# A routed-experts kernel on one core: another order of 21 tiles, and GpSimd in the manual schedule

## The chip, the core and the metric

The kernel runs on one core of one Trainium2 chip. The metric is the device time of one execution in microseconds, as a median of several runs. One execution was also taken with the hardware profiler; durations in this text are from it, unless they are called medians of the runs.

## The reference

The input x has 16 rows of 512 tokens with 128 channels, in float32. Every token is normalized, and three things are added up: x itself, a linear attention with decay, and a mixture of four experts of which each token takes two.

```python
xn = layernorm(x)                                   # (16, 512, 128)
# attention: 32 channels, no softmax, a token looks at those after it
scores = einsum('btc,bsc->bts', xn @ q_w, xn @ k_w) * decay_weights
att = (einsum('bts,bsc->btc', scores, xn @ v_w) @ o_w.T) * out_scale
# experts
rw, sel = top_k(xn @ router_w + router_b + load_balancer, 2); rw = softmax(rw)
e0 = (silu(xn @ sw_w1) * (xn @ sw_w3)) @ sw_w2      # hidden width 512
e1 = gelu(((xn @ eq + b) @ wv + b) @ wo @ c1w + b) @ c2w + b     # 256
syn = xn @ syn_w + b
h2 = layernorm(syn + (syn @ wv + b) @ wo + b) * n1g + n1b
e2 = (layernorm(h2 + relu(h2 @ f1w + b) @ f2w + b) * n2g + n2b) @ gen_w + b
e3 = gelu(xn @ ml_w1 + b) @ ml_w2 + b               # 512
out = x + att + rw[0] * e[sel[0]] + rw[1] * e[sel[1]]
```

## The kernel before

**Rows.** Each of the 16 rows (512 tokens, four chunks of 128) is loaded, its moments are taken on VectorE (`stats`), the reciprocal root on GpSimd (`inv`, L484), the normalization on ScalarE (`norm`, L494), a transpose and a projection to q, k, v and router logits on TensorE (`turn`, `proj`). Four rows make a `Quad`, for which the attention is computed together: `keys`, `score`, `scored` (L659), `near`, `far`, `outputs`, and `total` (L718), which adds the result to x; then the row is stored to the output in HBM (L602).

**Lists.** Rows are routed in groups (`GROUPS`, 2, 2, 4, 4 and 4 rows). There is one list in HBM for each pair of experts, six in all. When a group is routed, GpSimd scatters its tokens with their weights and numbers to the lists by indirect DMAs, one for each chunk (`send`, L506, destination `lists`, 64 in all).

**Tiles.** A list is then worked off in tiles of up to four chunks: `LISTS` gives the pair and the chunks of its tiles. A tile is loaded from the list on SyncE's queue (`L`, L880), transposed (`T`, `TT`), its biases are written to an accumulator `o` on VectorE (`B`, L908 and L910), and the two experts of its pair are computed. Expert 0 is `ga`, `gb` (a_ps, b_ps), experts 1 and 3 are `H` (h_ps) and an activation on ScalarE (`A`, L939), expert 2 has two normalizations with a turn of z after each (`U`, `S`, `I`, `O`, `N`, `Zu`, `F`, `Zv`). `Y` is each expert's last product (y_ps), `J` adds it by weight to `o` on VectorE (L963). Finally GpSimd adds `o` to the output by an indirect DMA for each chunk (`X`, L506, destination `out_dram`, 66 in all). Each X waits for all 16 row stores. There are four buffers `o`, four `xg`, three `xT`, and one each of `h0`, `h1`, `h3`.

**The order.** No loop of the code runs in this order. All steps are put into a plan with `add`: engine, a cost in us, what they wait for, which buffers they take until when, and a rank. `emit` goes through it like a list scheduler: it looks for the step that can start first, and of those on the same engine that can start within 0.25 us of it, takes the one of the lowest rank. The order that comes out is written as the program, and the manual schedule keeps it on its engines. The ranks are 5 for each row, 12 for each tile, in the order of `TURN`, and the offsets in `AHEAD`:

```python
rank = 5.0 * (b + QUAD - 1) + AHEAD["quads"][b // QUAD]     # attention of the quad of row b
rank = 5.0 * b - AHEAD["rows"] - (120.0 if b < 2 else 0.0)  # row b
tiles[pair, i].steps(k, g, AHEAD["tiles"] + 12.0 * k)       # k-th tile of TURN
```

`TURN` names a tile (pair, number) and the group after whose scatters it may be loaded. Should a list have fewer tokens by then than the tile takes, or more at the end than its tiles hold, the flag `turns` lets a loop at the end compute all rows densely instead. The last three tiles (`LAST`) are joined in parts of half a tile. Constant products (`fill`, `busy`) keep TensorE going while it has nothing else.

Of the kernel before, what the change touches and what calls it, by code (L numbers as in the profile page):

```python
# [11 lines left out]
ALU = mybir.AluOpType  # L12
# [5 lines left out]
P = 128  # L18
# [8 lines left out]

LISTS = [
    ((0, 1), (3, 4, 4, 4)), ((0, 2), (3, 2)), ((0, 3), (4, 4)),
    ((1, 2), (3, 3, 4, 3)), ((1, 3), (2, 4, 3, 4, 4, 3)), ((2, 3), (3, 2)),  # L30
]
NL = len(LISTS)
LR = 16 * 512
# [2 lines left out]


TURN = [
# [4 lines left out]
]  # L43
FILL = 25

AHEAD = {"rows": -2.0, "tiles": 62.0, "biases": -5.0, "quads": (9.0, -36.0, -27.0, -27.0)}
LAST = 3


# [39 lines left out]
def decay_attention__plus__routed_experts(  # L89
# [10 lines left out]
    nc = tc.nc  # L100
# [37 lines left out]
    def buf(pool, kind, shape, name, by):  # L138

        tag = kind if pool is once else f"{kind}.{which(kind, by)}"  # L140
        return pool.tile(shape, F32, tag=tag, name=f"{kind}_{name}", bufs=1)

    lists = tc.dram_tile([NL * LR, PW], F32, name="lists")


    queue = {"on": False, "fixed": None, "moving": []}
    behind = mybir.DependencyInfo(mybir.DependencyClass.NoSync, mybir.DependencyReason.DATA)

    def queued(i, key=None):

        if queue["on"]:
            others = [q for q, k in queue["moving"] if k != key or key is None]
            for q in others or [queue["fixed"]]:
                if q is not None:
                    tc.add_manual_dep(i.ins, q, behind, reason="the order of the plan")
            if key:
                queue["moving"].append((i.ins.name, key))
            else:
                queue.update(fixed=i.ins.name, moving=[])
        return i  # L160

    def mm(o, lhsT, rhs, start=True, stop=True):
        nc.tensor.matmul(o, lhsT, rhs, start=start, stop=stop)  # L163
# [6 lines left out]
    plan = {}  # L170
# [113 lines left out]
    neg_half = const.tile([P, NC], F32, tag="neg_half", name="neg_half")  # L284
# [27 lines left out]

    def bounds():
        for l, (pair, sizes) in enumerate(LISTS):
            queued(nc.gpsimd.memset(limit[:, l : l + 1], float(l * LR + P * sum(sizes))))
            for g in range(NG):
                last = max((k for q, k, at in TURN if q == pair and at <= g < NG - 1), default=-1)
                queued(nc.gpsimd.memset(need[:, g, l : l + 1], float(l * LR + P * sum(sizes[: last + 1]))))

    limit = const.tile([P, NL], F32, tag="limit", name="limit")  # L320

    need = const.tile([P, NG, NL], F32, tag="need", name="need")
# [101 lines left out]
    d_col = const.tile([P, 1], F32, tag="d_col", name="d_col")  # L424
    d_far = const.tile([P, 1], F32, tag="d_far", name="d_far")
# [10 lines left out]
    add("d_col", V, 0.15, lambda: nc.vector.tensor_scalar(d_col, d_col, 0.5, 0.5, ALU.mult, ALU.add), ["d_tanh"], rank=-97.0)  # L436

    def squared():
        queued(nc.gpsimd.tensor_tensor(d_far, d_col, d_col, ALU.mult))
        for _ in range(6):  # L440
            queued(nc.gpsimd.tensor_tensor(d_far, d_far, d_far, ALU.mult))

    add("d_far", G, 1.9, squared, ["d_col"], rank=-95.0)
    add("powers", V, 0.5, lambda: nc.vector.tensor_tensor_scan(
        powers, d_col.to_broadcast([P, P + 1]), one, 0.0, ALU.mult, ALU.add), ["d_col"], rank=-95.0)
# [35 lines left out]

    def inverse(ve, n, pool, name):
        rstd = pool.tile([P, n], F32, tag=f"rstd{name[0]}", name=f"rstd_{name}", bufs=FEW.get(name[0], 1))
        queued(nc.gpsimd.tensor_tensor(rstd, ve, neg_half[:, :n], ALU.pow))  # L484
        return rstd

    def offset(mv, rstd, n, pool, name):
# [15 lines left out]

    def scatter(o, src, index, n, key, **how):

        i = queued(nc.gpsimd.indirect_dma_start(  # L506
            out=o, out_offset=bass.IndirectOffsetOnAxis(ap=index, axis=0),
            in_=src, in_offset=None, bounds_check=n - 1, oob_is_err=False, **how,
        ), key)
        tc.add_to_no_dep_group(key, i.ins)  # L510
        tc.declare_no_dep(i.ins, group=key, reason="each row of the table is written once at most")
        if key == "lists":
            tc.declare_no_dep(i.ins, group="loads", reason="a tile is loaded when all its rows are there")
# [47 lines left out]
    class Row:  # L561
# [8 lines left out]
        def inv(s):  # L570
            s.rstd = inverse(s.ve, NC, small, f"x_{s.b}")
# [148 lines left out]
    class Group:  # L720
# [5 lines left out]
        def number(s):  # L726
            s.pay = [buf(work, f"pay{s.m}", [P, NC * s.m, PW], f"{s.g}_{k}", running[0]) for k in range(s.n // (NC * s.m))]
            for k, pay in enumerate(s.pay):
                at = NC * (s.first + s.m * k)
                number = tok[:, at : at + NC * s.m].unsqueeze(2).to_broadcast([P, NC * s.m, PW - P - 2])  # L730
                queued(nc.gpsimd.tensor_copy(pay[:, :, P + 2 :], number))

        def entry(s, k):
            return s.pay[k // (NC * s.m)][:, k % (NC * s.m), :]
# [39 lines left out]
        def send(s, k):  # L774
            scatter(lists, s.entry(k), s.idx[:, k : k + 1], NL * LR, "lists")

    quads = []

    def attention(b, a):

        rank = 5.0 * (b + QUAD - 1) + AHEAD["quads"][b // QUAD]
        of = range(QUAD)
# [23 lines left out]
    for g, m in enumerate(GROUPS):  # L806
        q = Group(g, first, m)
        q.before, before = before, q
        add(f"tok{g}", G, 0.25, q.number, takes=[(f"pay{q.m}", [f"send{g}.{NC * q.m * i + k}" for k in range(NC * q.m)]) for i in range(m // q.m)], at=6.0, rank=-200.0)
        for b in range(first, first + m):  # L810
            k = NC * (b - first)
            r = Row(b, work, lambda c, k=k, q=q: q.entry(k + c)[:, :D])
            lg = q.lg[:, :, k : k + NC]
            rank = 5.0 * b - AHEAD["rows"] - (120.0 if b < 2 else 0.0)
            ends = [f"store{b}"]
# [29 lines left out]
            if b % QUAD == QUAD - 1:  # L845
                attention(q0, quads[-1])
        rank = 5.0 * (first + m) - AHEAD["rows"] - 50.0
        n = NC * m
# [7 lines left out]
        for k in range(n):  # L856
# [3 lines left out]
            add(f"send{g}.{k}", G, 1.28, lambda q=q, k=k: q.send(k), need_q, rank=rank + 20.0)  # L860
        first += m
    add("bounds", G, 1.3, bounds, ["send0.3"], rank=0.0)


# [3 lines left out]
    class Tile:  # L868
# [110 lines left out]
        def inv(s, key):  # L979
            s.rstd = inverse(s.ve, s.n, s.tmp, f"{key}_{s.name}")  # L980
# [29 lines left out]
        def send(s, c):  # L1010
            scatter(rows_of_out, s.o[:, c, :], s.to[:, c : c + 1], B * T, "out", compute_op=ALU.add)

        def steps(s, k, g, ranks):
# [6 lines left out]
            def step(q, eng, us, fn, after=(), takes=(), rank=0.0):  # L1020
                add(name(q), eng, us, fn, [name(a) if isinstance(a, str) else a for a in after],
                    [(kind, [name(e) for e in ends]) for kind, ends in takes], ranks + rank)
# [21 lines left out]
            step("to", V, 0.08, s.numbers, [(name("L"), 4.0)])  # L1044
            step("B", V, n * (0.2 if 0 in s.pair else 0.46), s.biases, [(name("L"), 4.0)], [("o", [f"X{c}" for c in range(n)])], AHEAD["biases"])
            if 0 in s.pair:
# [36 lines left out]
    tiles = {}  # L1083
# [5 lines left out]
    for k, (pair, i, g) in enumerate(TURN):  # L1089
        tiles[pair, i].steps(k, g, AHEAD["tiles"] + 12.0 * k)  # L1090

    E = mybir.EngineType
    with tc.manual_schedule(engines={E.PE, E.DVE, E.Activation, E.SP}):
        queue["on"] = True
        emit()
        queue["on"] = False


    f = "p g l -> p (g l)"
# [141 lines left out]
```

## Time and profile before

| | |
|---|---|
| median of 3 runs | 345.11 us (343.02 to 345.42) |
| profiled execution, its own time | 307.28 us |
| its span, first to last instruction | 305.6 us |
| mean granted TensorE clock | 0.992 |
| PE busy | 288.4 us, 94% |
| DVE busy | 203.4 us, 67% |
| POOL busy | 203.7 us, 67% |
| ACT busy | 160.1 us, 52% |
| bytes moved | 26.55 MB |

PE is TensorE, PEld its weight loads, DVE VectorE, ACT ScalarE, POOL GpSimd and SP SyncE. A row of instructions gives the line of the kernel, the engine, the operation, what is written and read (`out<-in`), and how many; behind it stand busy time and the mean duration of one, and in brackets or last the idle time ahead of it with what ended it. A float32 product is two instructions in these records. The runs' median is some 38 us above the profiled execution's time.

### The profile page before, as it was taken

The numbers are of one execution on the slowest core, as the hardware profiler recorded it, in microseconds if no ns is written. First come the engines' busy times: TensorE is split into PE (matmuls) and PEld (weight loads), VectorE is DVE, ScalarE is ACT, GpSimd is POOL, SyncE is SP. The second block draws the span as 40 slices with busy tenths as digits, with TensorE's granted clock in tenths as the row PEclk, the third lists the DMA queues.
The fourth block names the chain that finished last, engine by engine and source line by source line (L and its number), as shares of the span: only waits on it lengthen the run. The fifth ranks groups of instructions, "written<-read, shape, count | busy, mean of one in ns | idle before, by whom it ended". The sixth has DMA issues, their size and how long they took to land.

```text
span 305.6 us, 6546 instructions
## 1 busy us (share of the span) xinstructions
PE 288.4 (94%) x2218; PEld 223.5 (73%) x2218; DVE 203.4 (67%) x827; ACT 160.1 (52%) x347; POOL 203.7 (67%) x238
## 2 busy tenths in 40 slices
PE   8999999899989999999979999999999999999970
PEld 7899777778765768775848888747847797765960
DVE  3888899899687497839597676428747237635330
ACT  2899896866951327735363765424444326517020
POOL 5648878778877778888847668884643448084472
PEclk9999999999999999999999999999999999999996
DMA  6994183915331261336323233553213223022032
GB/s 173 291 312 170 46 249 110 297 55 179 107 99 58 90 187 55 60 34 103 29 26 52 22 85 47 74 78 29 33 18 57 47 28 56 9 27 26 8 30 22
DMA packets 33237, 26.55 MB, mean 87 GB/s; under 512 B 3633, under 2 KB 30513, under 8 KB 33073
## 3 DMA queue, kind: packets, MB, share of 16 engines
q0 software_dynamic: 11552, 8.92, 19.7%
q1 hardware_dynamic: 21072, 16.44, 18.5%
q10 hardware_dynamic: 576, 0.74, 0.9%
q8 instruction: 19, 0.31, 0.4%
q14 instruction: 18, 0.14, 0.2%
HBM read 12.09 MB, written 14.12 MB: 86 GB/s over the span
## 4 chain that ended last, share of the span: by engine, by line
PE 66%; DVE 16%; DMA 6%; POOL 4%; issue 3%; ACT 2%; ACTq 0%; POOLq 0%; SPq 0%; DVEq 0%
PE y_ps L163 24%; PE h_ps L163 14%; PE a_ps L163 7%; PE b_ps L163 7%; PE f_ps L163 7%; DMA fold_sb<-in_fold_dram 2%; DVE sc L659 2%; POOL out_dram L506 2%; DMA out_dram<-o,to 2%; POOL rstd_x L484 2%; PE xT_ps L501 2%; PE proj_ps L163 1%; DVE st_x L475 1%; DVE o L963 1%; DVE x L718 1%
## 5 line engine op out<-in xcount | busy, mean ns | idle before, releaser
L506 POOL DMA_INDIRECT out_dram<-o,to x66 | 102.9, 1559 | 51.2 <-DVE o L963 37.2
L506 POOL DMA_INDIRECT lists<-pay,idx x64 | 63.3, 990 | 18.4 <-issue 6.4
L963 DVE SCALAR_TENSOR_TENSOR o<-y_ps,xg,o 128x128 f32<-128x128 f32 x132 | 38.3, 344 | 47.5 <-PE y_ps L163 47.1
L163 PEld LDWEIGHTS y_ps<-main_sb,h 128*128 128x128 f32 x456 | 53.9, 192 | 5.4 <-issue 3.8
L163 PE MATMUL y_ps<-main_sb,h 128*128 128x128 f32 x456 | 54.9, 275 | 0.3 <-ACT kT L647 0.3
L939 ACT ACTIVATE h<-h_ps,cols_sb 128x512 f32<-128x512 f32 (+2 forms) x40 | 24.4, 613 | 30.4 <-PE h_ps L163 29.7
L163 PE MATMUL h_ps<-xT,main_sb 128*128 128x512 f32 (+2 forms) x80 | 34.1, 522 | 1.4 <-DVE x L718 1.0
L939 ACT ACTIVATE h<-h_ps,b_e 128x512 f32<-128x512 f32 (+2 forms) x28 | 17.6, 628 | 24.9 <-PE h_ps L163 24.6
L922 ACT ACTIVATE th<-a_ps 128x512 f32<-128x512 f32 (+2 forms) x32 | 17.2, 542 | 23.8 <-PE a_ps L163 20.9
L163 PE MATMUL a_ps<-xT,w_sb 128*128 128x512 f32 (+2 forms) x64 | 29.2, 543 | 0.0
L494 ACT ACTIVATE pay<-x,off_x,rstd_x 128x128 f32<-128x128 f32 x64 | 26.3, 487 | 2.9 <-DVE off_x L489 2.3
L163 PEld LDWEIGHTS y_ps<-sw_w2h,h 128*128 128x128 f32 x224 | 26.1, 192 | 1.2 <-issue 0.4
L163 PE MATMUL y_ps<-sw_w2h,h 128*128 128x128 f32 x224 | 26.8, 276 | 0.0
L163 PE MATMUL b_ps<-xT,w_sb 128*128 128x512 f32 (+2 forms) x64 | 26.0, 541 | 0.3 <-ACT xT L890 0.3
L925 DVE SCALAR_TENSOR_TENSOR th<-th,a_ps 128x512 f32<-128x512 f32 (+2 forms) x32 | 19.4, 616 | 9.8 <-ACT th L922 9.5
L163 PE MATMUL h_ps<-xT,w_e 128*128 128x512 f32 (+2 forms) x56 | 25.1, 539 | 0.0
L484 POOL TENSOR_TENSOR rstd_x<-ve_x,neg_half 128x4 f32<-128x4 f32 x16 | 16.6, 1040 | 9.2 <-DVE ve_x L479 7.0
L908 DVE TENSOR_SCALAR o<-rows_sb,xg 128x128 f32<-128x128 f32 x66 | 15.2, 304 | 9.0 <-DMA out_dram<-o,to 8.9
L163 PEld LDWEIGHTS h_ps<-xT,main_sb 128*128 128x128 f32 x80 | 13.9, 191 | 9.3 <-issue 4.5
L930 DVE TENSOR_TENSOR h<-th,b_ps 128x512 f32<-128x512 f32 (+2 forms) x32 | 19.4, 618 | 1.2
L163 PEld LDWEIGHTS b_ps<-xT,w_sb 128*128 128x128 f32 x64 | 11.7, 190 | 10.0 <-issue 6.5
L163 PEld LDWEIGHTS a_ps<-xT,w_sb 128*128 128x128 f32 x64 | 11.1, 190 | 7.8 <-issue 5.0
(185 smaller groups left out, 489.9 us busy)
## 6 DMA issues: line engine op xcount, KB each, us to landing
x<-in_x_dram SPq DMA_DIRECT2D x16, 256.0 KB, 6.3
out_dram<-x SPq DMA_DIRECT2D x16, 256.0 KB, 3.5
xg<-lists SPq DMA_DIRECT2D x9, 288.0 KB, 2.8
xg<-lists SPq DMA_DIRECT2D x8, 216.0 KB, 2.5
main_sb<-in_main_dram SPq DMA_DIRECT2D x1, 1216.0 KB
out_dram<-o,to POOLq DMA_INDIRECT x66, 3.3
lists<-pay,idx POOLq DMA_INDIRECT x64, 2.3
lists<-none SPq DMA_DIRECT2D x6, 144.0 KB, 5.1
```

The lines of the kernel that those rows point to most:

```text
L163: nc.tensor.matmul(o, lhsT, rhs, start=start, stop=stop)
L484: queued(nc.gpsimd.tensor_tensor(rstd, ve, neg_half[:, :n], ALU.pow))
L494: nc.scalar.activation(o(c), v(c), AF.Identity, bias=off[:, c : c + 1], scale=rstd[:, c : c + 1])
L501: nc.tensor.transpose(pt[:, ts(c, P)], z(c), ident)
L506: i = queued(nc.gpsimd.indirect_dma_start(out=o, out_offset=bass.IndirectOffsetOnAxis(ap=index, axis=0), in_=src, in_offset=None, bounds_c ...
L659: nc.vector.tensor_tensor(s.sc[i], s.sbanks[i].rearrange("p (c t) -> p c t", c=NC), near.unsqueeze(1).to_broadcast([P, NC, P]), ALU.mult,)
L908: nc.vector.tensor_scalar(o, bias, w(c), None, ALU.mult)
L922: nc.scalar.activation(s.th[i], s.ga[i], AF.Tanh, scale=0.5)
L925: nc.vector.scalar_tensor_tensor(s.th[i], s.th[i], 1.0, s.ga[i], ALU.add, ALU.mult)
L930: nc.vector.tensor_tensor(s.h0[:, i, :], s.th[i], s.gb[i], ALU.mult)
L939: nc.scalar.activation(getattr(s, key)[:, i, :], s.hb[key, i], func, bias=bias[:, i : i + 1])
L963: nc.vector.scalar_tensor_tensor(o, s.py[e, chunks[0]][:, c, :], w(c), o, ALU.mult, ALU.add)
```

## The change

The tables of tiles are others. There are 21 tiles instead of 20 with the same 66 chunks and the same chunks for each pair; the list (1, 2) begins with a tile of one chunk, and the list (1, 3) ends in tiles of 2, 1 and 2. `TURN` has another order and other groups, and `AHEAD` other offsets. GpSimd joins the engines of the manual schedule; the helper `queued`, which ordered its instructions by added dependencies, is removed. In that helper each GpSimd instruction depended on those before it, except that scatters with the same destination had no order among themselves between two others.

```diff
 LISTS = [
     ((0, 1), (3, 4, 4, 4)), ((0, 2), (3, 2)), ((0, 3), (4, 4)),
-    ((1, 2), (3, 3, 4, 3)), ((1, 3), (2, 4, 3, 4, 4, 3)), ((2, 3), (3, 2)),
+    ((1, 2), (1, 4, 4, 4)), ((1, 3), (4, 4, 3, 4, 2, 1, 2)), ((2, 3), (3, 2)),
 ]
 TURN = [
-    ((1, 2), 0, 1), ((1, 3), 0, 0), ((0, 1), 0, 1), ((0, 2), 0, 3), ((0, 1), 1, 2), ((1, 2), 1, 2),
-    ((1, 2), 2, 4), ((1, 2), 3, 4), ((0, 1), 2, 3), ((2, 3), 0, 3), ((1, 3), 1, 2), ((1, 3), 2, 2),
-    ((0, 1), 3, 4), ((2, 3), 1, 4), ((0, 3), 0, 3), ((1, 3), 3, 3), ((0, 2), 1, 4), ((1, 3), 4, 4),
-    ((0, 3), 1, 4), ((1, 3), 5, 4),
+    ((1, 2), 0, 0), ((1, 3), 0, 1), ((0, 1), 0, 1), ((1, 3), 1, 2), ((1, 2), 1, 2), ((0, 1), 1, 2),
+    ((2, 3), 0, 3), ((0, 1), 2, 3), ((2, 3), 1, 4), ((0, 1), 3, 4), ((1, 3), 2, 3), ((0, 2), 0, 3),
+    ((1, 2), 2, 3), ((1, 3), 3, 4), ((0, 3), 0, 3), ((1, 3), 4, 4), ((0, 2), 1, 4), ((1, 2), 3, 4),
+    ((1, 3), 5, 4), ((0, 3), 1, 4), ((1, 3), 6, 4),
 ]
-AHEAD = {"rows": -2.0, "tiles": 62.0, "biases": -5.0, "quads": (9.0, -36.0, -27.0, -27.0)}
+AHEAD = {"rows": -4.0, "tiles": 56.0, "biases": 27.0, "quads": (-6.0, -84.0, -51.0, 15.0)}
...
-    queue = {"on": False, "fixed": None, "moving": []}
-    behind = mybir.DependencyInfo(mybir.DependencyClass.NoSync, mybir.DependencyReason.DATA)
-    def queued(i, key=None):
...
-        queued(nc.gpsimd.tensor_tensor(rstd, ve, neg_half[:, :n], ALU.pow))
+        nc.gpsimd.tensor_tensor(rstd, ve, neg_half[:, :n], ALU.pow)
...
-    with tc.manual_schedule(engines={E.PE, E.DVE, E.Activation, E.SP}):
-        queue["on"] = True
+    with tc.manual_schedule(engines={E.PE, E.DVE, E.Activation, E.Pool, E.SP}):
         emit()
-        queue["on"] = False
```

More of the change, by code (lines that the diff above doesn't have):

```diff
@@ L143, in decay_attention__plus__routed_experts @@
     lists = tc.dram_tile([NL * LR, PW], F32, name="lists")
-    queue = {"on": False, "fixed": None, "moving": []}
-    behind = mybir.DependencyInfo(mybir.DependencyClass.NoSync, mybir.DependencyReason.DATA)
-    def queued(i, key=None):
[L151 to L160, printed above, removed]
     def mm(o, lhsT, rhs, start=True, stop=True):
@@ L314, in bounds @@
         for l, (pair, sizes) in enumerate(LISTS):
-            queued(nc.gpsimd.memset(limit[:, l : l + 1], float(l * LR + P * sum(sizes))))
+            nc.gpsimd.memset(limit[:, l : l + 1], float(l * LR + P * sum(sizes)))
             for g in range(NG):
                 last = max((k for q, k, at in TURN if q == pair and at <= g < NG - 1), default=-1)
-                queued(nc.gpsimd.memset(need[:, g, l : l + 1], float(l * LR + P * sum(sizes[: last + 1]))))
+                nc.gpsimd.memset(need[:, g, l : l + 1], float(l * LR + P * sum(sizes[: last + 1])))
     limit = const.tile([P, NL], F32, tag="limit", name="limit")
@@ L438, in squared @@
     def squared():
-        queued(nc.gpsimd.tensor_tensor(d_far, d_col, d_col, ALU.mult))
+        nc.gpsimd.tensor_tensor(d_far, d_col, d_col, ALU.mult)
         for _ in range(6):
-            queued(nc.gpsimd.tensor_tensor(d_far, d_far, d_far, ALU.mult))
+            nc.gpsimd.tensor_tensor(d_far, d_far, d_far, ALU.mult)
     add("d_far", G, 1.9, squared, ["d_col"], rank=-95.0)
@@ L504, in scatter @@
     def scatter(o, src, index, n, key, **how):
-        i = queued(nc.gpsimd.indirect_dma_start(
+        i = nc.gpsimd.indirect_dma_start(
             out=o, out_offset=bass.IndirectOffsetOnAxis(ap=index, axis=0),
             in_=src, in_offset=None, bounds_check=n - 1, oob_is_err=False, **how,
-        ), key)
+        )
         tc.add_to_no_dep_group(key, i.ins)
@@ L730, in number @@
                 number = tok[:, at : at + NC * s.m].unsqueeze(2).to_broadcast([P, NC * s.m, PW - P - 2])
-                queued(nc.gpsimd.tensor_copy(pay[:, :, P + 2 :], number))
+                nc.gpsimd.tensor_copy(pay[:, :, P + 2 :], number)
         def entry(s, k):
```

## The prediction

> **What bounds the kernel now.** I read the page first, then busy time by stretches, then the chain of waits, then single tiles.
>
> ```profile
> span 305.6 us, 6546 instructions
> PE 288.4 (94%) x2218; PEld 223.5 (73%) x2218; DVE 203.4 (67%) x827; ACT 160.1 (52%) x347; POOL 203.7 (67%) x238
> ...
> PE   8999999899989999999979999999999999999970
> ...
> DVE  3888899899687497839597676428747237635330
> ```
>
> Only 17.2 us of the span (305.6 less 288.4) has no matmul in it. About 9 us of that is the tail, in the last two slices. 94% busy also holds products on constants: the groups of fill_ps (6.8 us) and busy_ps (6.6 us) do no work of the reference, so TensorE is short of work in the first 30 us. After that it is the bound. Where the rest of the idle time lies comes from busy time by stretches (PE is the second column of times):
>
> ```profile
> core 0: us, PE busy (x) PEld busy (x) DVE busy (x) ACT busy (x) POOL busy (x), PEclk, DMA share, GB/s
> 50.00:57.00 7.00, 5.98 (x65) 5.30 (x66) 5.73 (x23) 6.23 (x13) 5.71 (x6) 1.00 0.73 215
> 85.00:92.00 7.00, 5.98 (x82) 4.75 (x81) 6.01 (x30) 4.31 (x12) 5.24 (x6) 1.00 0.34 105
> 107.00:121.00 14.00, 14.00 (x97) 10.27 (x90) 12.36 (x40) 5.94 (x13) 10.60 (x11) 1.00 0.39 123
> 121.00:147.00 26.00, 26.00 (x145) 18.42 (x144) 18.85 (x61) 14.61 (x28) 21.88 (x15) 1.00 0.47 66
> 147.00:156.00 9.00, 7.28 (x43) 5.10 (x42) 6.11 (x29) 4.01 (x8) 7.82 (x6) 1.00 0.34 31
> 156.00:290.00 134.00, 133.28 (x786) 100.59 (x786) 77.69 (x276) 60.25 (x115) 75.97 (x53) 1.00 0.30 40
> ```
>
> Idle in TensorE: 1.02 us at 50-57, 1.02 at 85-92, nothing from 107 to 147, 1.72 at 147-156, and 0.72 in the 134 us after that. The same view in steps of 10 us gives 1.41 at 30-50. All that a better order could save between 30 and 290 us is thus about 6 us, at a granted clock of 1.00 throughout. The one large stall stands in the chain of waits, the tile rows tell what GpSimd does around it:
>
> ```profile
> 147.77 3.36 DMA out_dram<-o,to
> 151.25 0.95 DVE o L908 x4
> 154.42 1.66 ACT z L494 x4
> ...
> 233.15 7.14 PE y_ps L163 x64
> 240.29 3.44 PE h_ps L163 x8
> ```
>
> ```profile
> L506 POOL DMA_INDIRECT out_dram<-o,to x66: 1532/1542/1797, 121.0 to 297.9; - x66
> L506 POOL DMA_INDIRECT lists<-pay,idx x64: 966/972/1212, 22.1 to 119.7; - x64
> ```
>
> GpSimd writes the 64 list scatters until 120.7, and only then the first of 66 output scatters, one each 1.84 us (1.54 and about 0.30 between two). There are four buffers o, so the bias step of the eighth tile (L908) needs the output of the fourth. The timeline of 146-157 us shows VectorE idle for 2.82 us on that, and off_u of another tile queued behind it (154.24); ScalarE then normalizes at 154.42, and TensorE stands at the turn of z.
>
> **The change, part by part. GpSimd's order.** The helper queued already chains GpSimd's instructions in the order of the plan; only scatters of the same kind may change places. Under the manual schedule that freedom goes. No instruction is added. A row for two swapped scatters doesn't exist; the nearest is one scatter slot, so between -1.84 and +1.84 us, and I take 0: scatters of one group wait in sequence for their rows, so the order by number is also that of readiness.
>
> **Work of TensorE.** 66 chunks of 128 rows before and after, with the same pairs (15, 5, 8, 13, 20, 5), so every product with 128 moving columns is there as often. Only the wide ones are cut otherwise. Two tiles have one chunk: (1,2) with four such products, (1,3) with six; each is two instructions in the records, 20 in all. In the chain above, 64 instructions of y_ps at 128 columns take 7.14 us, 112 ns each; 8 of h_ps at 512 take 3.44, 107.5 ns for each 128 columns. Extra: 20 x 4 ns = 0.08 us. The Trainium skill speaks against such tiles (page "TensorE: Matmul & The Clock Gate", section "Back-to-back issue gap"): with the weight loads counted it states 81 ns sustained at 128 columns and 131 at 512, so 81 - 33 = 48 ns lost per 128 columns, and 20 x 48 = 1.0 us. The row decides: it has these very float32 products, with their weight loads beside them. I take +0.1. The 21st tile's load is one more issue of 0.32 us on SyncE's queue, its copies on ScalarE (52% busy) and VectorE some 0.2 us each in fixed cost; they lie beside matmuls.
>
> **The first tiles.** By the sizes of the loads on SyncE's queue, (1,3) with 2 chunks is loaded at 36.69, then the first two tiles of the second group at 48.68 and 51.64. I count the work of a tile in products of one chunk, 0.215 us (two of 107.5 ns): with its transposes a chunk is 16.5 for (0,1), 11.5 for (1,2), 12.5 for (1,3), 19.5 for (0,2), 15.5 for (2,3). Before, the first group brings 2 x 12.5 = 25 and the second (3 of (1,2), 3 of (0,1)) 84; after, 11.5 and then 4 of (1,3) and 3 of (0,1), 99.5. The sum is the same (109 and 111, 24 us), but less is there at 50 us. The early tile's h_ps at 51.0, 51.5 and 52.0 are 1.3 us; one chunk of (1,2) has three products ready at once, 0.65. So +0.65 us in the stretch that is idle for 1.02 already. Bounds 0 and +1.3; I take +0.65.
>
> **The eighth tile's buffer.** The load sizes give the order before: 2, 3, 3, 4, 3, 4, 3 chunks. The first four tiles hold 12 chunks and the first seven 318 products. After: 1, 4, 3, 4, 4, 4, 3, so 12 chunks and 319.5. The output of the fourth tile comes at the same time (121 + 12 x 1.84 and some inverses, then 3.3 to land: 151), and TensorE is equally far. But the eighth tile is now (0,1), and AHEAD puts its biases at +27 instead of -5, behind the other VectorE work of two tiles. What was queued behind the waiting instruction (off_u, for which ScalarE and then TensorE waited) goes ahead. Bounds: 0 and all 1.72 us; I take -1.2. The next buffers come easier: the ninth tile is there after 16 chunks (159), when TensorE has 385 products of eight tiles instead of 364 to do first.
>
> **Biases late.** The +27 acts on the first tiles as well, where VectorE is not idle: it is busy 8.36, 9.72 and 9.47 us of each 10 from 50 to 80, 2.45 us free. The Y products of a tile wait for its biases, and h0, h1, h3 have one buffer each. Between 0 (if they fall into gaps) and the 5.7 us of the first rival below; nearer to 0, since Y is also late for lack of h there, so +1.0.
>
> **Attention.** Quads 0 to 2 go earlier (AHEAD -6, -84, -51), but each begins when its fourth row is projected: nothing. Quad 3 falls from rank 48 to 90, behind tiles of 56, 68 and 80. Before, it is ready at 85.5 (first k_ps), when by the timeline's matmuls 20 of the 24 us of those first three tiles are done. Its stores leave at 108.4 to 110.9 and land by 114, GpSimd needs them at 121: 7 us of cover. Bounds 0 and +4 (stores 11 us later); I take 0.
>
> **The tail.** The last tile had 3 chunks and has 2.
>
> ```profile
> 294.25 1.54 POOL L506 DMA_INDIRECT out_dram<-o,to  x1 [0.86 <-DVE o L963]
> ...
> 296.10 1.54 POOL L506 DMA_INDIRECT out_dram<-o,to  x1 [0.30 <-DVE o L963]
> ...
> 297.95 1.54 POOL L506 DMA_INDIRECT out_dram<-o,to  x1 [0.31 <-issue]
> ```
>
> TensorE ends its last Y at 295.75 and the last scatter starts 2.2 us later, as three follow on GpSimd at 1.84. With two, TensorE needs 4.4 us after the tile before it, and GpSimd is still busy for 4.2 with that tile's four chunks: the scatters start at 4.5 and 6.35, 1.95 after the last Y. Gain 0.25 us; without the backlog 1.5. I take -0.25. The drain and barrier after it (6 us) stay.
>
> **The sum.** +0.1 + 0.65 - 1.2 + 1.0 - 0.25 = +0.3 us on the execution of 307.28 (span 305.6, 1.7 around it). The runs' median is 345.11, 1.123 times that; the profile doesn't show where those 38 us lie. At either scale 0.3 stays under 0.4: **345.5 us**. A measurement of this kernel can tell about 1%, 3.5 us (its three runs spread over 2.4), from no change.
>
> **Rivals.** First, slower: **late biases starve TensorE at 55-85 us.** The first three tiles' biases are 5 chunks at 0.62 and 3 at 0.28 (L908, L910), 3.9 us against 2.45 free on VectorE. If they wait until the rows are through at 80, the 36 y_ps before that (4.0 us) move behind it, and with h1 held, a pair of wide h_ps too (1.7): +5.7, 350.8. It decides from about 3.5 us of new idle time there. For it: VectorE's 97% at 60-70. Against: attention and rows give TensorE other work. Second, slower: **output scatters begin late**, because quad 3 is last. From the end of the first seven tiles TensorE has some 9 us of the eighth's hidden products, so a start at 121 + d costs d less that cover; stores 11 us later cost at most 4: 349. Third, faster: **the stalls go and none come**: 1.72 + 0.72 + 1.02 + 1.02 and the tail's 0.25, 4.7: 340.4. For it: TensorE has equal work at hand by groups; against: it needs all at once. That a list holds fewer rows than a tile takes, and the dense loop runs, I exclude: routing the given inputs by the reference gives every tile of the new TURN its rows (tightest (1,2) to its third tile, 1190 for 1152).
>
> **Chances.** Forecast 0.46 (own range 342.5 to 348.3), late biases 0.29, late scatters 0.11, stalls gone 0.14. The range 340 to 352.5 takes in the third rival and the first with its error. Faster by over 1% 0.14, within 1% 0.46, slower 0.40.
>
> **What would show it.** Right: PE busy near 288 us; idle at 147-156 under 0.6 us; no wait of L908 for out_dram over 2 us; first output scatter within 3 us of 121; last one 2 us after the last y_ps. Wrong: over 3 us of idle in 55-85, with y_ps waiting for o (L908), or the first output scatter after 125.

## The result: 356.6 us, and the profile after

The kernel after takes **356.62 us** (356.07 to 357.26, 4 runs), the kernel before beside it 344.15 us (343.02 to 345.42, 4 runs): ratio **1.0362 [1.0312, 1.0412]**, 12.5 us slower. The forecast was 345.5, and its range ended at 352.5. One thing has to be known to read what follows: the same kernel before takes about 345 us in some sets of runs and about 308 in others, so every ratio below is between runs of one set, taken together on one chip.

The page of the kernel after; its lines are 17 lower than those of before, since the helper `queued` is gone (L489 is the scatter, L146 the matmul, L946 the sum by weight):

```profile
span 355.5 us, 6557 instructions
PE 308.4 (87%) x2230; PEld 236.5 (67%) x2230; DVE 202.0 (57%) x828; ACT 161.4 (45%) x354; POOL 203.4 (57%) x238
...
PE   8998829879952396699999999999999999999990
...
PEclk9999967958975588689999999999999999999997
```

TensorE has 47 us without a matmul instead of 17, and the second row shows where: slices 5 to 17, that is 36 to 151 us. From slice 18 on it is as full as before. The granted clock is lower in nearly the same slices (6 to 18). DVE, ACT and POOL are busy for as long as before (202.0, 161.4 and 203.4 us, against 203.4, 160.1 and 203.7): the work is the same, and it waits. TensorE's own busy time is 20.0 us longer (308.4 against 288.4) for nearly the same products, so the 49.9 us of longer span are 30 us of idle time and 20 of products that run slower. Busy time by stretches, in the windows that the prediction read:

```profile
core 0: us, PE busy (x) PEld busy (x) DVE busy (x) ACT busy (x) POOL busy (x), PEclk, DMA share, GB/s
50.00:57.00 7.00, 5.42 (x65) 4.55 (x65) 3.79 (x20) 5.58 (x16) 1.48 (x18) 0.50 0.25 76
85.00:92.00 7.00, 6.95 (x54) 3.92 (x53) 6.75 (x34) 5.97 (x13) 4.64 (x7) 1.00 0.54 168
107.00:121.00 14.00, 2.23 (x4) 0.64 (x3) 1.18 (x5) 1.09 (x3) 7.77 (x8) 0.50 0.13 47
121.00:147.00 26.00, 20.94 (x155) 15.53 (x156) 12.73 (x51) 7.41 (x18) 10.69 (x11) 0.83 0.13 43
147.00:156.00 9.00, 8.06 (x77) 5.20 (x77) 2.43 (x6) 2.33 (x4) 0.00 (x0) 0.64 0.10 26
156.00:290.00 134.00, 133.49 (x766) 97.95 (x765) 86.24 (x301) 64.68 (x122) 85.49 (x61) 1.00 0.36 53
```

At 107-121, where the earlier profile had 14.00 us of matmuls, there are now 2.23. The two scatter rows give the same from GpSimd's side (first and last start are the two numbers ahead of the semicolon):

```profile
L489 POOL DMA_INDIRECT lists<-pay,idx x64: 966/971/1296, 21.8 to 173.6; - x64
...
L489 POOL DMA_INDIRECT out_dram<-o,to x66: 1532/1542/1707, 174.9 to 347.5; - x66
```

The first output scatter starts at 174.9 instead of 121.0, 53.9 us later. The last one starts 172.6 us after it, against 176.9 before. So all of the loss lies ahead of the first output scatter, while rows are routed.

What happens there is seen best in the timeline from 96 to 121 us, of which I show one row of each kind (start, duration, engine, then what ended the idle time in brackets):

```profile
99.42 0.97 POOL L489 DMA_INDIRECT lists<-pay,idx  x1 [0.30 <-issue]
...
101.40 0.58 PE L146 MATMUL proj_ps<-w_all,xnT 128*128 128x100 f32 x4 [1.04 <-issue]
...
109.94 0.80 PE L146 MATMUL b_ps<-xT,w_sb 128*128 128x384 f32 x1 [1.11 <-issue]
...
116.00 0.97 POOL L489 DMA_INDIRECT lists<-pay,idx  x1 [0.30 <-issue]
119.82 1.13 DVE L946 SCALAR_TENSOR_TENSOR o<-y_ps,xg,o 128x128 f32<-128x128 f32 x4 [20.47 <-remote]
119.91 0.48 ACT L576 COPY qkv<-proj_ps 128x384 f32<-128x384 f32 x1 [22.52 <-remote]
```

GpSimd issues list scatters one each 1.27 us (0.97 and 0.30) without a break until 116.97. The products proj_ps end at 102, and y_ps ends at 99.4; but ScalarE, which copies proj_ps, and VectorE, which adds y_ps, go on only at 119.9, about 3 us after the run of scatters. TensorE meanwhile issues a matmul now and then, with idle time put down to "issue". None of the semaphore updates by which TensorE tells that it is done is recorded from 97.15 to 119.80; then seven follow within 0.28 us. Of its 442 updates in the whole program 418 are recorded, so these came late and are not just missing from the trace. I call such a stretch a **hold**. The waits of the whole execution show them under a releaser that the profile of before did not have ("remote": an update is recorded, and no instruction that ended just ahead of it):

```profile
ACT qkv L576 <- remote: 22.5, 1, 22.5
DVE o L946 <- remote: 20.5, 1, 20.5
...
ACT h L922 <- remote: 14.2, 1, 14.2
...
ACT S L666 <- remote: 6.9, 1, 6.9
```

The columns are total, times and longest, in us. All such waits of VectorE and ScalarE sum to 77 us here. The profile of before on which the prediction stands has none.

### The profile page after: what moved, and what is told of

It is laid out like the page before. It is cut to its first block, busy times and chain, and to the rows that moved or that the text cites. A ratio compares the mean times of both kernels' runs of the same rounds, so it can differ in the third digit from the quotient of the medians.

```text
span 355.5 us, 6557 instructions
## 1 busy us (share of the span) xinstructions
PE 308.4 (87%) x2230; PEld 236.5 (67%) x2230; DVE 202.0 (57%) x828; ACT 161.4 (45%) x354; POOL 203.4 (57%) x238
## 4 chain that ended last, share of the span: by engine, by line
PE 75%; another core or an unknown queue 8%; ACT 7%; issue 4%; DMA 2%; DVE 1%; ACTq 0%; POOL 0%; POOLq 0%; DVEq 0%
PE y_ps L146 22%; PE h_ps L146 14%; PE a_ps L146 6%; PE f_ps L146 6%; PE b_ps L146 6%; PE proj_ps L146 4%; PE sc_ps L146 3%; ACT pay L477 3%; DMA fold_sb<-in_fold_dram 2%; PE xT_ps L484 2%; PE at_ps L146 2%; PE u_ps L146 2%; PE fill_ps L146 1%; PE nt_ps L146 1%
## 5 line engine op out<-in xcount | busy, mean ns | idle before, releaser
L489 POOL DMA_INDIRECT out_dram<-o,to x66 | 102.8, 1557 | 51.0 <-DVE o L946 35.0
L489 POOL DMA_INDIRECT lists<-pay,idx x64 | 63.5, 992 | 34.1 <-issue 15.8
L946 DVE SCALAR_TENSOR_TENSOR o<-y_ps,xg,o 128x128 f32<-128x128 f32 x132 | 37.9, 344 | 66.2 <-PE y_ps L146 45.5
L146 PEld LDWEIGHTS y_ps<-main_sb,h 128*128 128x128 f32 x456 | 53.6, 192 | 2.6 <-issue 1.4
L146 PE MATMUL y_ps<-main_sb,h 128*128 128x128 f32 x456 | 55.3, 275 | 0.0
L922 ACT ACTIVATE h<-h_ps,cols_sb 128x512 f32<-128x512 f32 (+3 forms) x44 | 25.1, 580 | 44.7 <-PE h_ps L146 29.8
L146 PE MATMUL proj_ps<-w_all,xnT 128*128 128x100 f32 x128 | 19.8, 306 | 18.4 <-ACT xnT L567 16.9
L146 PE MATMUL h_ps<-xT,main_sb 128*128 128x512 f32 (+3 forms) x88 | 34.5, 494 | 1.1 <-issue 1.1
L146 PEld LDWEIGHTS proj_ps<-w_all,xnT 128*128 128x128 f32 x128 | 18.1, 218 | 21.5 <-ACT xnT L567 19.4
L146 PE MATMUL y_ps<-sw_w2h,h 128*128 128x128 f32 x224 | 29.4, 285 | 3.2 <-issue 3.1
L146 PEld LDWEIGHTS y_ps<-sw_w2h,h 128*128 128x128 f32 x224 | 28.1, 201 | 5.4 <-issue 4.9
L922 ACT ACTIVATE h<-h_ps,b_e 128x512 f32<-128x512 f32 (+3 forms) x30 | 17.9, 600 | 30.1 <-PE h_ps L146 29.7
L146 PE MATMUL a_ps<-xT,w_sb 128*128 128x512 f32 (+2 forms) x64 | 29.2, 543 | 0.0
L146 PE MATMUL b_ps<-xT,w_sb 128*128 128x512 f32 (+2 forms) x64 | 27.2, 552 | 1.5 <-issue 1.5
L146 PE MATMUL h_ps<-xT,w_e 128*128 128x512 f32 (+3 forms) x60 | 27.7, 556 | 0.0
L908 DVE SCALAR_TENSOR_TENSOR th<-th,a_ps 128x512 f32<-128x512 f32 (+2 forms) x32 | 19.5, 616 | 11.8 <-ACT th L905 10.5
L146 PEld LDWEIGHTS h_ps<-xT,main_sb 128*128 128x128 f32 x88 | 16.0, 196 | 10.4 <-issue 7.7
L467 POOL TENSOR_TENSOR rstd_u<-ve_u,neg_half 128x4 f32<-128x4 f32 (+3 forms) x8 | 7.3, 917 | 26.2 <-DVE ve_u L462 25.8
L576 ACT COPY qkv<-proj_ps 128x384 f32<-128x384 f32 x16 | 7.7, 481 | 28.5 <-remote 22.5
```

Source lines behind the costliest of these rows:

```text
L489: i = nc.gpsimd.indirect_dma_start(out=o, out_offset=bass.IndirectOffsetOnAxis(ap=index, axis=0), in_=src, in_offset=None, bounds_check=n ...
L576: nc.scalar.copy(qkv, s.pbank[:, :, : 3 * CH].rearrange("p c (k d) -> p c k d", d=CH))
L908: nc.vector.scalar_tensor_tensor(s.th[i], s.th[i], 1.0, s.ga[i], ALU.add, ALU.mult)
L922: nc.scalar.activation(getattr(s, key)[:, i, :], s.hb[key, i], func, bias=bias[:, i : i + 1])
L946: nc.vector.scalar_tensor_tensor(o, s.py[e, chunks[0]][:, c, :], w(c), o, ALU.mult, ALU.add)
```

## The experiments

**Theory.** In the usual executions TensorE's completions are held while list scatters run without a break; the profiled execution of before was one without holds; the new tables make the holds longer. **Rivals:** the order of GpSimd under the manual schedule (the other half of the change); a worse order of work in itself (late biases, late stores), which would cost the same with or without holds.

**Before again, and the two halves of the change.** Three kernels in one set (before beside them: 346.03 us). The first is before, unchanged. The second has before's tables and the new schedule:

```diff
-    with tc.manual_schedule(engines={E.PE, E.DVE, E.Activation, E.SP}):
+    with tc.manual_schedule(engines={E.PE, E.DVE, E.Activation, E.Pool, E.SP}):
...
-        queue["on"] = True
```

The third has the new `LISTS`, `TURN` and `AHEAD`, and keeps `queued`.

> The kernel before, unchanged, to see it in the executions that take 344 us; the profiled one took 307. Theory A (TensorE's completions are held up while GpSimd issues list scatters without a break, and which executions meet it depends on timing): if this execution takes about 344, its trace shows one or more stretches between 40 and 150 us with TensorE idle or crawling, all engines waiting, some 35 us together, each ending 1 to 3 us after a run of list scatters ends. Theory B (the 38 us are around the span or in a lower clock over the whole of it): the trace has the span of 305 to 308 again, or a longer one spread evenly over all stretches.

> Of the change only GpSimd's place in the manual schedule, with the tables of before; the order of the instructions differs from before in one pair of output scatters. Theory A and B and the prediction: no change, 342 to 347 us. If GpSimd's order were the cause of the loss: 355 or more.

> Of the change only the tables (tiles, their order, the offsets), with the helper that orders GpSimd as before. All theories that lay the loss on the new order of the work: 354 to 359 us, as with the whole change. If the manual schedule is needed for the loss: 344.

Before: 343.9 us. This profile, of a usual execution, is the one that the prediction lacked:

```profile
span 342.2 us, 6546 instructions
...
L506 POOL DMA_INDIRECT out_dram<-o,to x66: 1532/1542/1803, 157.9 to 334.6; - x66
```

```profile
20.00:60.00 40.00, 33.91 (x444) 29.32 (x444) 28.52 (x145) 27.68 (x70) 27.36 (x64) 0.91 0.45 145
60.00:100.00 40.00, 34.30 (x322) 27.15 (x320) 27.88 (x122) 25.65 (x60) 25.20 (x28) 0.96 0.35 109
100.00:150.00 50.00, 33.46 (x256) 22.24 (x256) 22.01 (x68) 9.54 (x21) 20.72 (x22) 0.80 0.20 65
150.00:290.00 140.00, 137.76 (x820) 104.21 (x819) 90.53 (x328) 68.03 (x129) 93.67 (x68) 1.00 0.35 48
```

The first output scatter is at 157.9 instead of 121.0, 36.9 us later, and the span is 36.6 us longer. TensorE idles 28.3 us from 20 to 150, against 3.7 in the profile of the prediction. Before has holds as well (42 us of "remote" waits), and in this phase lie the 38 us that the prediction left unexplained: 12.3 of them as longer busy time of TensorE (300.7 us against 288.4), the rest as idle time. The manual schedule alone takes 341.61, ratio 0.988 [0.9833, 0.9927]; its instruction order differs from before's in one exchanged pair of output scatter groups. The tables alone take 357.87, ratio 1.0338 [1.0293, 1.0383], which is the whole change. The rival of GpSimd's order falls, for executions with holds.

**A pause between scatters.** The kernel after, with an operation of 1.0 us on GpSimd behind every fourth list scatter, whose result nobody reads:

```diff
             scatter(lists, s.entry(k), s.idx[:, k : k + 1], NL * LR, "lists")
+            if k % 4 == 3:
+                nc.gpsimd.tensor_tensor(pause, ones[:, :NC], neg_half, ALU.pow)
```

> The kernel after, with a small GpSimd instruction of 1.0 us (the power of a 128x4 tile, its result unused) after every fourth list scatter. Theory A (unbroken list scatters hold TensorE's completions): the stretches without work between 40 and 150 us become shorter, 335 to 350 us, though GpSimd has 16 us more to do. Rival (late biases and the order alone starve TensorE at 40 to 150 us): the stretches stay, and with the later scatters the time grows to 357 to 370.

**324.48 us**, ratio 0.9388 [0.9344, 0.9433] in that same set: more work on GpSimd, and 32 us less time than the kernel after (the tables alone took 357.87 in this set). The stretch of 100 to 150 us has 44.20 us of matmuls instead of 28.29:

```profile
100.00:150.00 50.00, 44.20 (x296) 29.08 (x296) 28.37 (x89) 17.86 (x34) 37.54 (x36) 0.93 0.27 72
```

"Remote" waits fall from 77 to 14 us, and the first output scatter starts at 142.7. So the rival of a worse order in itself, which foresaw 357 to 370 here, falls too.

**What in the pause does it?** The second set was meant to part time from number. Before with the same pause; after with a pause behind every second scatter; with all of a group's pauses behind its last scatter; with an operation of 0.1 us in the pause's place:

```diff
-            if k % 4 == 3:
-                nc.gpsimd.tensor_tensor(pause, ones[:, :NC], neg_half, ALU.pow)
+            if k % 4 == 3:
+                nc.gpsimd.memset(pause[:, 0:1], 0.0)
```

> The kernel before with the same pause of 1.0 us after every fourth list scatter. Theory A (both orders lose time only because unbroken list scatters hold TensorE up, before some 36 us of it and after some 50): 318 to 327 us, within 4 us of the paced kernel after (324.5). Rival (before suffers from something else, or the order of after is itself worse by 12 us): 335 or more, or 308 to 314.

> The kernel after with the pause after every second list scatter, 32 pauses. Theory A: the rest of the held stretches goes too, 312 to 322 us. Rival (one pause in four is already enough and GpSimd's own length counts): 326 to 340, because the output scatters begin some 16 us later.

> The kernel after with the same 16 pauses, but all of a group's behind its last list scatter, so that they lengthen GpSimd's work as much and break no run. Theory A: the held stretches stay, 353 to 372 us. Rival (what helped was only that later work came later): 320 to 330, as with the spread pauses.

> The kernel after with a one-element-wide memset (0.1 us) instead of the pause after every fourth list scatter. If any other instruction between scatters releases TensorE: 320 to 330 us. If it is the time without a new scatter that matters: 350 to 358.

On this occasion before took 308.14 us, and no profile of the set has a "remote" wait of VectorE or ScalarE. The questions were not answered: 315.33 and 301.04 lie outside all that was expected, and 322.89 lies in the theory's range, and 330.3 in its rival's, by luck, since there was no hold to shorten. But another question was: what the kernels do without holds.

| kernel | us | ratio |
|---|---|---|
| before, paused every fourth | 322.89 | 1.0487 [1.0447, 1.0526] |
| after, paused every second | 330.3 | 1.0734 [1.0694, 1.0773] |
| after, pauses at the end of a group | 315.33 | 1.0249 [1.0207, 1.0291] |
| after, 0.1 us every fourth | 301.04 | 0.9786 [0.9751, 0.9822] |

Without holds the pause is pure cost, and the new tables, here with the 0.1 us operations, are 2.1% *faster* than before. The cost is an ordinary wait: the plan doesn't know the pauses, GpSimd falls behind, and an inverse root for a tile stands behind list scatters. In the kernel paused every second scatter it reads so:

```profile
140.56 0.16 DVE L473 SCALAR_TENSOR_TENSOR off_u<-mv_u,rstd_u 128x4 f32<-128x4 f32 x1 [12.44 <-POOL rstd_u L468]
```

The releaser has a name there, POOL's rstd_u. In a hold it is "remote", and the instruction that was waited for had ended long before.

**The same once more, with holds.** In the third set before took 346.45 us.

> The kernel after, unchanged, beside before on another occasion. So far before took 344 to 346 us beside some runs and 308 beside others, and after was only seen beside 344. If after's loss belongs to the held stretches alone, then where before takes about 308 after takes 299 to 303 (as with the tiny memset, 301.0), and where before takes 344 to 346 after takes 355 to 359. If after's order is slower in itself: 315 or more beside a before of 308.

> The tiny memset after every fourth list scatter once more. Where before takes 308: 300 to 303, equal to after. Where before takes 345: if it is the time without a new scatter that matters, 350 to 358; if any other instruction between releases TensorE, 320 to 330.

> After with the 1.0 us pause after every fourth list scatter, once more. Where before takes 345: 322 to 327 as seen. Where before takes 308 there is nothing to release, and 16 us more of GpSimd ahead of the output scatters costs 12 to 16 us over after: 313 to 317.

> After with all pauses of a group behind its last list scatter, once more. Where before takes 308: 314 to 317 as seen. Where before takes 345: if unbroken runs hold TensorE up, 355 to 372; if only later work helped, 320 to 330.

After: 356.9 us, 1.0297 [1.0232, 1.0362]. With 0.1 us every fourth: 357.14, 1.0301 [1.0244, 1.0357]. With 1.0 us every fourth: 324.69, 0.9351 [0.928, 0.9421], with 27 us of "remote" waits left. With the pauses at the end of the groups: 352.32, 1.0188 [1.012, 1.0256], below the 355 to 372 expected. So neither another instruction between scatters nor the same pauses in one place helps much; time without a scatter, spread among them, does. The kernel with 0.1 us is the cleanest pair of the study, the same program in two sets. Its stretch of 100 to 150 us with holds, and then without:

```profile
100.00:150.00 50.00, 25.49 (x177) 18.85 (x175) 14.65 (x56) 9.20 (x21) 24.54 (x31) 0.69 0.17 56
```

```profile
100.00:150.00 50.00, 49.81 (x278) 35.26 (x277) 31.74 (x111) 23.01 (x43) 41.10 (x38) 1.00 0.40 76
```

It takes 357.14 us in one and 301.04 in the other, 56.1 apart; before differs by 38.3 between the same two sets (346.45 and 308.14). The new tables gain 7.1 us where there are no holds, and lose 17.8 more to them where there are: 10.7 us slower. The two sets ran on two chips (1 and 10), and the kernel after itself was never met without holds; with them it takes what this one takes (356.9 and 357.14).

**Which part of the tables?** The old tiles with the new offsets, the new tiles with the old offsets, the pause in the last two groups only, and the dense pause again:

```diff
--- before
+++ this run
-AHEAD = {"rows": -2.0, "tiles": 62.0, "biases": -5.0, "quads": (9.0, -36.0, -27.0, -27.0)}
+AHEAD = {"rows": -4.0, "tiles": 56.0, "biases": 27.0, "quads": (-6.0, -84.0, -51.0, 15.0)}
...
--- after
+++ this run
-AHEAD = {"rows": -4.0, "tiles": 56.0, "biases": 27.0, "quads": (-6.0, -84.0, -51.0, 15.0)}
+AHEAD = {"rows": -2.0, "tiles": 62.0, "biases": -5.0, "quads": (9.0, -36.0, -27.0, -27.0)}
...
--- after
+++ this run
-            if k % 4 == 3:
+            if k % 4 == 3 and s.g >= 3:
```

> The old tiles and their order (LISTS, TURN) with the new offsets (AHEAD). My theory: the holds come from long runs of list scatters, and the offsets decide how closely the rows, and so the groups' scatters, follow one another. If the offsets carry the longer holds, this takes 352 to 360 us where the kernel before takes 345; if the tiles carry them, 343 to 348. Where the kernel before takes 308 us there are no holds, and this takes 300 to 310. Rival (the time is lost by a worse order of work, not by holds): the same loss on both occasions.

> The new tiles and their order with the old offsets. The other half of the run with the new offsets: if the offsets carry the longer holds, 343 to 348 us beside a kernel before of 345; if the tiles carry them, 352 to 360. Beside 308: 300 to 312. If both halves lie between, each carries a part.

> The kernel after, with the pause of 1.0 us behind every fourth list scatter in the last two groups only (groups 3 and 4, 32 of the 64 scatters). My theory: the longest holds (97 to 120 us, 133 to 148 us) lie there, those before 76 us stay, some 15 us. Where the kernel before takes 345 us: 325 to 340, less than the kernel after by at least 17. Where it takes 308: 306 to 312. If the holds were spread evenly, half of the 32 us that the pause everywhere saved: 341.

> The kernel after, with the pause behind every second list scatter. It took 330.3 us where the kernel before took 308. My theory: with twice the time without a scatter no hold is left, so it takes the same 328 to 333 on an occasion where the kernel before takes 345. If the holds depend on the number of scatters and not on their pace, it takes 345 or more there.

> The old tiles with the new offsets once more; beside a kernel before of 308 us it took 310. Where the kernel before takes 345 us: 352 to 360 if the offsets carry the changed kernel's longer holds, 343 to 348 if the tiles carry them. Where it takes 308 again: 310.

> The new tiles with the old offsets once more; beside a kernel before of 308 us it took 309. Where the kernel before takes 345 us: 343 to 348 if the offsets carry the longer holds, 352 to 360 if the tiles carry them. Where it takes 308 again: 309.

Both sets had no holds (before 308.11 and 307.42 us). New offsets with old tiles: 310.04 and 309.67, ratios 1.0075 [1.0045, 1.0106] and 1.0074 [1.0053, 1.0094]. Old offsets with new tiles: 308.88 and 309.37, 1.002 [0.9999, 1.0041] and 1.0058 [1.0036, 1.0081]. Paused in the late groups: 306.63, 0.9966 [0.9949, 0.9984]. Paused every second: 330.69, 1.0722 [1.068, 1.0763], as in the second set. So without holds neither half has the 2% gain of the two together. Busy time by stretches shows a part of why: from 20 to 100 us TensorE idles 3.7 us in before, 2.0 with the new offsets and 5.2 with the new tiles alone; from 100 to 290 us it idles 2.4 in before, 5.0 with the new offsets alone and 1.1 with the new tiles. Each half mends one end and spoils the other. Both together have 2.3 and 0.5. These are 3.3 us less idle time than in before; the rest of the 7.1 us is not explained by it. Which half makes the holds longer these runs could not show, nor whether late or denser pauses end them.

## Why the prediction was wrong

**The base of the sum.** This is the step that failed: "The runs' median is 345.11, 1.123 times that; the profile doesn't show where those 38 us lie. At either scale 0.3 stays under 0.4". The 38 us are not a scale. They are holds in the list-scatter phase, which depend on how the work lies beside the scatters, and the change moves all of that work. Their size was open to the change by its whole amount in both directions; it went from about 38 to about 56 us (56.1 measured with the 0.1 us operations). No rival held this, since none had a cause that the profile of 307.28 us does not show. With 38 us unexplained in 345, a range of 12 us could not be justified.

**GpSimd's order, 0.** Right, as far as it was run: the swap of a pair costs nothing in an execution with holds (341.61 beside 346.03 is not slower).

**The steps within TensorE's work** can be held only against an execution without holds. I use the kernel with 0.1 us every fourth scatter at 301.04 us, which is the kernel after but for 16 operations of about 0.1 us each. Its windows and rows (the bias step is L894 there and L908 in before, whose row stands first):

```profile
50.00:57.00 7.00, 6.54 (x98) 5.72 (x96) 6.35 (x34) 5.76 (x15) 6.15 (x7) 1.00 0.54 171
85.00:92.00 7.00, 7.00 (x112) 5.45 (x110) 6.87 (x29) 4.09 (x12) 5.57 (x8) 1.00 0.32 100
...
147.00:156.00 9.00, 9.00 (x50) 6.54 (x49) 8.10 (x21) 6.09 (x14) 7.48 (x6) 1.00 0.40 41
156.00:290.00 134.00, 133.66 (x812) 103.57 (x811) 82.41 (x294) 63.65 (x128) 80.60 (x57) 1.00 0.31 40
```

```profile
DVE o L908 <- DMA out_dram<-o,to: 8.9, 3, 5.9
...
DVE o L894 <- DMA out_dram<-o,to: 0.8, 1, 0.8
```

```profile
289.54 1.54 POOL L490 DMA_INDIRECT out_dram<-o,to  x1 [0.43 <-DVE o L949]
291.39 1.54 POOL L490 DMA_INDIRECT out_dram<-o,to  x1 [0.30 <-DVE turns L1092]
```

- **Small products, +0.1.** All of TensorE's busy time is 285.7 us, no more than before's 288.4, so no cost shows. But a term of 0.1 us, or of an estimated 1.0 us by the Trainium skill's "Back-to-back issue gap" (page "TensorE: Matmul & The Clock Gate"), can't be isolated beside differences of several us; which of the two was the better price stays open.
- **First tiles, +0.65.** Sign wrong: in the stretch of 50 to 57 us, for which it was priced, TensorE idles 0.46 us instead of 1.02, and from 30 to 60 us 2.23 instead of 2.43.
- **Eighth tile's buffer, -1.2.** Right in place and sign. The waits of the bias step for out_dram fall from 8.9 us in three to 0.8 in one, and the 1.72 us of idle time at 147-156 become none.
- **Biases late, +1.0.** Too large: from 55 to 85 us the idle time goes from 0.22 to 0.37. The first rival (late biases, +5.7) is refuted, where there are no holds. In the kernel after its sign, over 3 us of idle time in 55-85, did come (4.01 us), but no product y_ps waits there for o: the holds made the sign come, not late biases.
- **Attention, 0, and the second rival.** Quad 3 was not late: the last row is stored at 102.4 instead of 110.3, and the first output scatter starts at 119.1. In the kernel after it does start late (174.9, past the 125 named as a sign of error), but the same order stores at 102.4 without holds, so the stores are late by the holds and not by the rank of quad 3.
- **Tail, -0.25.** The last two rows above: GpSimd has nearly no backlog, and the last scatter starts 1.2 us after TensorE's last Y (290.2), where before needed 2.2. So -1.0, near the 1.5 that the prediction gave for no backlog.

Without holds these terms sum to some -4 us: -0.2, -1.7, +0.15 and -1.0, with -1.0 at 85-92 and -0.4 at 156-290, which the prediction had left to its third rival ("the stalls go", -4.7). The measured difference is -7.1 (308.14 to 301.04). TensorE's busy time between 20 us and its last Y is 2.3 us less (267.4 against 269.7), which no step explains; the ends of matmuls are modelled in these records, and I leave it open. Thus without holds the third rival, which had a chance of 0.14, comes nearest (-4.7 said, -7.1 measured); with holds none of the cases does.

## What to carry to other kernels

Before a sum is made on one profiled execution, its own time has to agree with the runs' median; where it is 11% away, the difference is the largest unknown of the case, and the first thing to find is a profile of a usual execution. Read "remote" as a releaser, with idle time of "issue" between single matmuls, as a sign that completions may come late: here such waits sum to 14 to 77 us in the profiles with holds, and to none in the others. An order tuned to 1% can lose more by where it meets runs of indirect scatters than it gains by filling stalls, and the pace of those scatters is then a knob of its own.

## What the runs showed of the hardware that was not expected

- Runs of indirect scatters on GpSimd, one each 1.27 us, go with holds of TensorE's completions of up to 22.6 us (97.15 to 119.80, 15 scatters). The long ones of the kernel after end at 50.3, 119.8 and 148.0, which is 1.3, 2.8 and 1.9 us after the last scatter of a run; but not all do: in the usual execution of before one ends at 104.76, within a run from 94.6 to 112.2. That a pause of 1.0 us after four scatters takes 32 us off the same kernel in two sets (324.48 and 324.69, against 356.9) shows that the pace of the scatters has part in it.
- What holds the updates up is not settled. The hold does not end with a fetch of instructions: in the kernel after the last DMA packets that bring instructions start at 96.7 us and the next at 133.5, and the work goes on at 119.8 without one. The data isn't slow either: in the kernel with 0.1 us a packet of GpSimd's scatters takes 86 ns on average without holds and 85 with them, a packet of the other loads and stores 43 and 44. But records are missing in executions with holds, above all those of DMAs that have landed: 1949 are recorded with holds and 3101 without, for the same transfers of that kernel. Each run here comes with a span and a clock, which are records too, so whether recording itself has part in the holds is a rival that no run tests.
- The scatters alone are not enough. In the first profile of before 25 of them follow one another from 80 to 112 us with no hold, at the same 0.97 and 0.30 us. Three of the sets had holds in every kernel, the least with the 1.0 us pause (before at 344 to 346 us), three had none (307 to 308). The number of the chip doesn't tell them apart: both the first set of experiments and the last name chip 8, the one with holds and the other without. What does is open.
- The granted clock is low in the held stretches and shortly after them (0.50 at 107-121, a mean of 0.64 at 147-156), and is 1.00 again from 156 us. It follows the idle time there: from 97.2 to 102.4 us it is still 1.00, while products already stand apart, and then 0.50 until 126.2, some 6 us after the hold. It also falls without a hold. In the kernel paused every second scatter TensorE stands for 13.36 us on the ordinary wait shown above, and the clock goes down one slice (8.2 us) later than its busy time:

```profile
PE   7899987897998995079999999999999999999990
...
PEclk9999699799999999569999999999999999999996
```

So a low clock doesn't mark a hold. What it adds to the loss isn't parted by these runs. In the kernel with 0.1 us, 18.5 of the 56.8 us between its two spans are busy time of TensorE (304.2 against 285.7); what the low clock adds to the products themselves is within this part.

- No kernel is best in both: among those run, the tables with 0.1 us operations at 301.04 us without holds, and the 1.0 us pause at 324.5 with them (about 15 us too many where there are none, by before's 322.89 against 308.14). The pause in the late groups alone takes 306.63 without holds, no more than before's 308.11, but 5.6 more than with the 0.1 us; with holds it was not seen.
